# Expert tiles: token numbers in a small tile of their own, biases loaded apart from the matrices and ahead of them

## The chip, the cores and the metric

The kernel runs on one core of one Trainium2 chip. The metric is the device time of one execution in microseconds (us), the median of several runs. The profile is one execution taken by the hardware profiler; its span, 1414.2 us, is close to the median of the runs, 1411.49 us.

## The reference

A network of two layers works on a picture of 2 x 256 x 48 x 48. Only its last part is touched here, a mixture of experts over B*N = 2 * 2304 = 4608 tokens of C = 256 numbers:

```
gate_logits = xf @ Wg + bg
top_w, top_i = top_k(gate_logits, 2);  top_w = softmax(top_w)
w_dense[token, e] = top_w of the expert e, else 0
for e in range(8):
    h = gelu(xf @ W1[e] + b1[e])              # 256 -> 1024
    out += w_dense[:, e] * (h @ W2[e] + b2[e])  # 1024 -> 256
```

Each token goes to two of the eight experts, so 9216 rows of token and expert have to be worked through. Everything is float32.

## The kernel before

The stages ahead (a local attention with a convolution, then a state-space layer with the gate) fill the first 838 us and are not touched. The gate writes each normalised token twice into a table in memory, `xs`, sorted by expert. A row of `xs` has XW = C + E + 1 = 265 numbers: the token's 256, its weight for each of the 8 experts, and in the last column the token's own number.

`experts` works through this table in tiles. A pair tile has 256 rows (2 halves of 128), a single tile 128. There are 36 pair tiles and, among them, 4 single ones; further single tiles stand behind a branch that is only taken when the counts demand it. Two tables computed on the chip (`plan`) say where the rows of each tile begin and which expert they belong to, so the loads use addresses from registers.

For tile i:

- `fetch(i)` (L1752) issues two loads on the queue of SyncE: the rows into `ex` (265 KB for a pair, four buffers) and the whole weights of the expert into `wt` (2184 KB, three buffers). A row of `wt` holds, per partition, W1 (2048 numbers), W2 (2048), then b1 (8), b2 (256) and a mask of the expert (8): WCOL = 4368 in all. The first tile's weights lie in a buffer of their own that is filled long before.
- `turn(i)` (L1767) transposes the rows on TensorE (L895), copies them to `ext` on VectorE (L897), and works out each row's weight: `own` is the product of the row's eight gate weights with the mask from `wt` (L1777), `weight` is their sum (L1781).
- `up(i)` (L1811) is the first matrix: 32 matmuls into PSUM (L1820), and on ScalarE a Gelu with b1 added into `hid` (L1824).
- `weight_sums(i)` (L1793 to L1796) and `hidden_sums(i)` (L1805 to L1808) form on VectorE the sums `ts` and `ss` of blocks that a seven-product scheme for two-by-two blocks needs. `ts` and `ss` have one buffer each.
- `down(i)` (L1837) is the second matrix: for a pair tile the seven products in the order p1, p7, p2, p4, p5, p6, p3, 8 matmuls each (L1859). p7 needs the sum s3, p5 needs s1, p6 needs s2 and p3 needs s4. VectorE then adds the products up into the results `ey` (L1864 to L1870) and adds b2 (L1872). For a single tile, 16 plain matmuls (L1846) and one addition (L1847).
- `finish` (L1826) scales a half's result by its weight on ScalarE (L1829) and adds it to the tokens' rows of `acc` in memory with an indirect DMA on GpSimd (L1831): "the scatter". The rows' numbers are the last column of `ex`, so `ex` stays in use until the scatter has landed.

`run` (L1886) calls them in this order, and loads three tiles ahead:

```
up(i); turn(i + 1); hidden_sums(i); down(i); weight_sums(i + 1); fetch(i + 3)
```

A scheduler places the instructions of each engine in this neighbourhood, and each engine then runs its own list strictly in order; a buffer that is used again makes the instruction that writes it wait for its former readers. The loads on SyncE keep their program order, so a load that waits holds up the loads behind it. The scheduler puts `own` of a tile far forward on VectorE: ahead of the `ts` of the tile before it and of the results of the tile before that.

Of the kernel before, what the change touches and what calls it, by code (L numbers as in the profile page):

```python
# [31 lines left out]
F32 = mybir.dt.float32  # L32
I32 = mybir.dt.int32
AF = mybir.ActivationFunctionType
ALU = mybir.AluOpType
AX = mybir.AxisListType

P = 128
B, C, H, W = 2, 256, 48, 48
N = H * W  # L40
NH = C // P
# [29 lines left out]
E, HID = 8, 1024  # L71
NHC = HID // P
# [5 lines left out]
NUSUAL = E // 2  # L78
NROWS = E * PART + TR
XW = C + E + 1  # L80
WCOL = NH * HID + NHC * C + NHC + C + E
F32_EPS = float(np.finfo(np.float32).eps)


# [30 lines left out]
def bcast(ap, axis, shape):  # L115
    return ap.unsqueeze(axis).to_broadcast(shape)


class Flow:
# [12 lines left out]
    def add(self, key, engine, cost, make, needs=(), takes=(), uses=(), due=0, chain=None, mode=None):  # L132

        self.ops[key] = dict(engine=engine, cost=cost, make=make, needs=[n for n in needs if n], takes=takes,
                             uses=[u for u in uses if u], due=due, chain=chain, mode=mode)
# [87 lines left out]
class Kernel:  # L225
# [1496 lines left out]
    def experts(self, ctx):  # L1722
        nc, ins = self.nc, self.ins
        self.psum(ctx, 4, 2)
        hp = self.pool("eh", 2, ctx)
        ew = self.pool("ew", 3, ctx)
# [4 lines left out]
        fetched, turned, hidden, sums = {}, {}, {}, {}  # L1731
# [19 lines left out]

        def fetch(i):  # L1752
            halves, n = tiles[i]
            x = hp.tile([P, 2, XW], F32, tag="ex", name="ex", bufs=4)[:, :halves]
            if i == 0:
                self.tc.keep_in_program_order(nc.sync.dma_start(x, self.expert_rows(self.xs[0:TR, :])))
                fetched[i] = x, self.first_weights
                return
            at = where[2 - halves]
            row = self.value(at[0:1, 0, n : n + 1], sp, NROWS - TR)  # L1760
            part = self.value(at[0:1, 1, n : n + 1], sp, (E - 1) * P)
            nc.sync.dma_start(x, self.expert_rows(self.xs[bass.ds(row, halves * P), :]))
            wt = ew.tile([P, WCOL], F32, tag="wt", name="wt")
            self.tc.keep_in_program_order(nc.sync.dma_start(wt, ins["We"][bass.ds(part, P), :]))
            fetched[i] = x, wt

        def turn(i):  # L1767

            halves = tiles[i][0]
            x, wt = fetched[i]  # L1770
            xt = hp.tile([P, NH, halves * P], F32, tag="ext", name="ext")
            self.transposes(
                xt.rearrange("p k q -> p (k q)"),
                [x[:, j, k * P : (k + 1) * P] for k in range(NH) for j in range(halves)], nc.vector.tensor_copy,
            )
            own = hp.tile([P, halves, E], F32, tag="own", name="own")
            nc.vector.tensor_tensor(  # L1777
                own, x[:, :, C : C + E], bcast(wt[:, WCOL - E :], 1, [P, halves, E]), ALU.mult
            )
            weight = hp.tile([P, halves], F32, tag="weight", name="weight")  # L1780
            nc.vector.tensor_reduce(weight, own, AX.X, ALU.add)  # L1781
            turned[i] = xt, weight

        def weight_sums(i):

# [24 lines left out]

        def up(i):  # L1811
            rows = tiles[i][0] * P
            xt, wt = turned[i][0], fetched[i][1]
            w1 = wt[:, : NH * HID].rearrange("p (k o) -> p k o", k=NH)
            b1 = wt[:, WCOL - C - NHC - E : WCOL - C - E]
            hid = hidden[i] = hp.tile([P, NHC, rows], F32, tag="hid", name="hid")
            for c in range(NHC):
                ps = self.bank()
                for k in range(NH):
                    nc.tensor.matmul(  # L1820
                        ps[:, :rows], lhsT=w1[:, k, c * P : (c + 1) * P], rhs=xt[:, k, :],
                        start=k == 0, stop=k == NH - 1,
                    )
                nc.scalar.activation(hid[:, c, :], ps[:, :rows], AF.Gelu, bias=b1[:, c : c + 1])  # L1824

        def finish(i, y, j):  # L1826

            x, weight = fetched[i][0], turned[i][1]
            nc.scalar.activation(y, y, AF.Identity, scale=weight[:, j : j + 1])  # L1829
            token = x[:, j, XW - 1 :].bitcast(I32)  # L1830
            put = nc.gpsimd.indirect_dma_start(  # L1831
                self.acc, bass.IndirectOffsetOnAxis(ap=token, axis=0), y, None, compute_op=ALU.add
            )
            self.tc.declare_no_dep(put.ins, group=f"tile{i}", reason="a token has one row of an expert")
            self.tc.add_to_no_dep_group(f"tile{i}", put.ins)

        def down(i):  # L1837
            wt, hid = fetched[i][1], hidden[i]
            w2 = wt[:, NH * HID : NH * HID + NHC * C].rearrange("p (k o) -> p k o", k=NHC)
            b2 = wt[:, WCOL - C - E : WCOL - E]  # L1840
            banks = self.ps2.tile([P, 2, 512], F32, tag="banks", name="po")
            if tiles[i][0] == 1:
                y = hp.tile([P, C], F32, tag="ey", name="ey", bufs=5)
                po = banks[:, 0, :C]
                for c in range(NHC):
                    nc.tensor.matmul(po, lhsT=hid[:, c, :P], rhs=w2[:, c, :], start=c == 0, stop=c == NHC - 1)  # L1846
                nc.vector.tensor_add(y, po, b2)  # L1847
                finish(i, y, 0)
            else:
                v = sums.pop(i)  # L1850
                p = {}

                for n, (name, a, w) in enumerate((
                    (1, "a11", "b11"), (7, "s3", "t3"), (2, "a12", "b21"), (4, "a22", "t4"), (5, "s1", "t1"),
                    (6, "s2", "t2"), (3, "s4", "b22"),
                )):
                    p[name] = banks[:, n // 4, n % 4 * P : (n % 4 + 1) * P]
                    for c in range(NHC // 2):
                        nc.tensor.matmul(p[name], lhsT=v[a][:, c], rhs=v[w][:, c], start=c == 0, stop=c == NHC // 2 - 1)  # L1859
                y0, y1 = (hp.tile([P, C], F32, tag="ey", name="ey", bufs=5) for _ in range(2))  # L1860
                p1, u2, u3, u4 = (hp.tile([P, P], F32, tag=f"u{j}", name=f"u{j}", bufs=1) for j in range(4))
                add = nc.vector.tensor_add
                nc.scalar.copy(p1, p[1])  # L1863
                add(y0[:, :P], p[2], p1)  # L1864
                add(u2, p[6], p1)
                add(u3, p[7], u2)
                add(u4, p[5], u2)
                add(y1[:, :P], p[4], u3)
                add(y1[:, P:], p[5], u3)
                add(y0[:, P:], p[3], u4)  # L1870
                for j, y in enumerate((y0, y1)):
                    add(y, y, b2)  # L1872
                    finish(i, y, j)
            del fetched[i], turned[i], hidden[i]

        fill(0)
        fetch(0)
        where, many = self.plan(plan)
        turn(0)
        for e in range(1, E):  # L1880
            fill(e)
        fetch(1)
        fetch(2)
        weight_sums(0)

        def run(first, end):  # L1886
            for i in range(first, end):
                up(i)
                if i + 1 < end:
                    turn(i + 1)  # L1890
                if tiles[i][0] == 2:
                    hidden_sums(i)
                down(i)
                if i + 1 < end:
                    weight_sums(i + 1)
                if i + 3 < end:
                    fetch(i + 3)
# [3 lines left out]
        with self.tc.If(self.value(many[0:1, 0:1], list(self.nc.engines), NSINGLE) > NUSUAL):  # L1901
            for i in range(usual, usual + 3):
                fetch(i)
            turn(usual)
            run(usual, len(tiles))
# [17 lines left out]
    def run(self):  # L1923
# [33 lines left out]
        nc.vector.tensor_copy(self.taken, self.c["base"])  # L1957
        self.first_weights = self.pool("ew0", 1).tile([P, WCOL], F32, name="wt")
        nc.sync.dma_start(self.first_weights, self.ins["We"][0:P, :])
# [37 lines left out]
def _arrays(i):  # L1997
# [29 lines left out]
        "W_in": w_in, "W_out": at("W_out").T,  # L2027
        "We": experts.reshape(E * P, WCOL),
        "vec": np.concatenate([vec[k] for k in _VEC], axis=1),
# [21 lines left out]
```

## Time and profile before

| | |
|---|---|
| median of 3 runs | 1411.49 us (1408.32 to 1415.42) |
| span of the profiled execution | 1414.2 us |
| TensorE, matmuls | 1269.9 us, 90% |
| VectorE | 1013.5 us, 72% |
| ScalarE | 780.4 us, 55% |
| GpSimd | 531.3 us, 38% |
| up, L1820, 1280 matmuls | 275.5 us |
| `wt` loads | 40 of 2184 KB |
| `ex` loads | 36 of 265 KB, 4 of 132.5 KB |
| scatters, L1831 | 76, 1559 ns each on GpSimd |

The shares are averages over very different stages. The stage in question begins at 838.43 us with the first matmul of `up` and ends for TensorE at 1374 us; behind it `acc` is read back, transposed and written out. What the change is worth has to be read from that stretch alone: which engine runs without a gap there, and which wait ends last in a tile. An engine's wait of many microseconds may cost nothing if another engine is never kept waiting by it. A line is a line of the kernel's program; where one helper serves many places (L895, L897) the names of the tiles tell them apart.

### The profile page before, as it was taken

The page shows a single profiled execution, that of the slowest core. Times are in us where ns is not written, and L with a number is a line of the kernel's source. Part 1 is how long each engine was busy: PE and PEld are TensorE (multiplying, and loading weights), DVE is VectorE, ACT ScalarE, POOL GpSimd, SP SyncE. Part 2 cuts the span into 40 slices and gives each one's busy share as a digit, 9 for nine tenths or more (in the row PEclk, how much of TensorE's full clock was granted, in tenths as well). Part 3 has the DMA queues.
Part 4 walks back from the last instruction along what each step waited for, and adds up shares of the span by engine and source line. Part 5 has one row for each costly group of instructions (what it writes and reads, how often), then busy time and mean ns, then how long its engine had stood idle before and what let it go on. Part 6 is the DMA issues. An engine that isn't in the chain of part 4 may idle for free.

```text
span 1414.2 us, 23686 instructions
## 1 busy us (share of the span) xinstructions
PE 1269.9 (90%) x8144; PEld 1012.9 (72%) x8144; DVE 1013.5 (72%) x2610; ACT 780.4 (55%) x1920; POOL 531.3 (38%) x648
## 2 busy tenths in 40 slices
PE   5999999998998899999988539998999999999983
PEld 4566767666666566666665429997998999998983
DVE  4999999997788889899978636654645645655653
ACT  2688877897987777777866212332332332432320
POOL 5213030111466777778676831221222222221220
PEclk9999999997999999999999859999999999999996
DMA  7321413121332233324243147666566667666628
GB/s 285 107 88 46 138 38 105 37 64 65 116 99 82 68 90 107 101 93 120 82 127 100 57 134 279 209 194 214 177 217 225 180 218 232 196 208 219 203 50 275
DMA packets 100442, 199.54 MB, mean 141 GB/s; under 512 B 10059, under 2 KB 86044, under 8 KB 94876
## 3 DMA queue, kind: packets, MB, share of 16 engines
q1 hardware_dynamic: 80540, 171.57, 36.4%
q0 software_dynamic: 14400, 19.74, 6.6%
q10 hardware_dynamic: 5380, 6.69, 1.4%
q8 instruction: 66, 1.08, 0.3%
q14 instruction: 56, 0.46, 0.1%
HBM read 158.71 MB, written 44.18 MB: 143 GB/s over the span
## 4 chain that ended last, share of the span: by engine, by line
PE 38%; DVE 15%; DMA 14%; ACT 3%; issue 3%; POOL 2%; another core or an unknown queue 0%; SPq 0%; DVEq 0%; ACTq 0%; POOLq 0%
PE bank L1820 11%; PE po L1859 10%; DMA wt<-in_We 7%; DMA acc<-ey,ex 5%; PE bank L909 4%; PE zbank L909 3%; PE bank L1420 2%; DVE xc L1106 2%; PE bank L895 1%; PE bank L1359 1%; PE bank L1402 1%; DVE mt L1322 1%; ACT mt L1314 1%; DVE y L1410 1%; POOL xs L1629 1%
## 5 line engine op out<-in xcount | busy, mean ns | idle before, releaser
L1820 PE MATMUL bank<-ext,wt 128*128 128x256 f32 (+1 forms) x1280 | 275.5, 373 | 10.0 <-ACT hid L1824 9.2
L1831 POOL DMA_INDIRECT acc<-ey,ex x76 | 118.5, 1559 | 435.0 <-ACT ey L1829 394.8
L1820 PEld LDWEIGHTS bank<-ext,wt 128*128 128x128 f32 x1280 | 233.0, 192 | 41.7 <-ACT hid L1824 11.7
L1824 ACT ACTIVATE hid<-bank,wt 128x256 f32<-128x256 f32 (+1 forms) x320 | 143.0, 462 | 83.0 <-PE bank L1820 79.0
L1863 ACT COPY u<-po 128x128 f32<-128x128 f32 x36 | 9.6, 266 | 226.6 <-PE po L1859 226.6
L1859 PE MATMUL po<-ts,ss 128*128 128x128 f32 x864 | 108.4, 275 | 0.0
L1859 PEld LDWEIGHTS po<-ts,ss 128*128 128x128 f32 x864 | 102.6, 192 | 0.0
L585 DVE SCALAR_TENSOR_TENSOR x<-hid,w2r,x 128x1128 f32<-128x1128 f32 (+3 forms) x72 | 99.9, 1392 | 0.4 <-ACT hid L579 0.2
L909 PE MATMUL bank<-xn,win 128*128 128x387 f32 x240 | 94.3, 517 | 1.1 <-DVE lg L1445 1.0
L1777 DVE TENSOR_TENSOR own<-ex,wt 128x16 f32<-128x16 f32 (+1 forms) x40 | 6.9, 173 | 122.9 <-DMA wt<-in_We 114.8
L674 POOL COPY kp<-kp 128x10 f32<-128x10 f32 (+1 forms) x60 | 23.4, 390 | 190.2 <-DVE kp L667 190.2
L793 ACT ACTIVATE prob<-prob,top 128x308 f32<-128x308 f32 x144 | 78.2, 549 | 17.4 <-DVE top L782 17.0
L1314 ACT ACTIVATE mt<-mt,cum 128x128 f32<-128x128 f32 x288 | 87.4, 392 | 0.0
L1106 DVE SCALAR_TENSOR_TENSOR xc<-bank,vec,xc 128x384 f32<-128x384 f32 x144 | 85.1, 605 | 2.4 <-ACT xc L1095 2.2
L909 PE MATMUL zbank<-xn,win 128*128 128x384 f32 x192 | 77.6, 529 | 4.2 <-ACT z L1216 4.2
L1629 POOL DMA_INDIRECT xs<-u,rows x72 | 71.9, 999 | 22.5 <-issue 16.7
L1859 PE MATMUL po<-wt,hid 128*128 128x128 f32 x576 | 77.5, 278 | 0.0
L1420 PE MATMUL bank<-wout,y 128*128 128x264 f32 x288 | 72.9, 398 | 2.6 <-DVE ss L1435 1.3
L1859 PEld LDWEIGHTS po<-wt,hid 128*128 128x128 f32 x576 | 71.7, 195 | 0.1
L824 PE MATMUL bank<-pt,val 110*64 110x128 f32 (+1 forms) x864 | 69.4, 278 | 0.8 <-ACT pt L814 0.8
L799 ACT ACTIVATE prob<-prob,rden 128x308 f32<-128x308 f32 x144 | 67.7, 547 | 4.3 <-DVE rden L848 4.2
L824 PEld LDWEIGHTS bank<-pt,val 110*64 110x64 f32 (+1 forms) x864 | 58.7, 136 | 14.7 <-issue 10.2
(288 smaller groups left out, 2982.7 us busy)
## 6 DMA issues: line engine op xcount, KB each, us to landing
wt<-in_We SPq DMA_DIRECT2D x40, 2184.0 KB
mt<-decays SPq DMA_DIRECT2D x36, 512.0 KB
ex<-xs SPq DMA_DIRECT2D x36, 265.0 KB
rd<-decays SPq DMA_DIRECT2D x68, 128.0 KB
val<-vtab SPq DMA_DIRECT2D x72, 110.0 KB
vraster<-vout SPq DMA_DIRECT2D x18, 256.0 KB
acc<-x SPq DMA_DIRECT2D x36, 128.0 KB
vtab<-vraster SPq DMA_DIRECT2D x12, 304.0 KB
```

The costliest lines, as they stand in the source:

```text
L585: nc.vector.scalar_tensor_tensor(dst, src, w[:, k : k + 1], dst, ALU.mult, ALU.add)
L793: nc.scalar.activation(t, t, AF.Exp, bias=T["top", c][:, a : a + 1], scale=-1.0, accum_out=T["den", c][:, a : a + 1])
L824: nc.tensor.matmul(po[j * HD : (j + 1) * HD, :P], lhsT=T["val", c][:nk, i, a * HD : (a + 1) * HD], rhs=T["pt", key][:nk, j, i, :], start=i ...
L909: self.nc.tensor.matmul(ps, lhsT=lhs(k), rhs=rhs(k), start=k == 0, stop=k == NH - 1)
L1106: nc.vector.scalar_tensor_tensor(out(), T["bank", ("cv", at)][:, i : i + TB], wc[:, i : i + 1], out(), ALU.mult, ALU.add)
L1314: nc.scalar.activation(t, t, AF.Relu, bias=at_s, scale=-1.0)
L1420: nc.tensor.matmul(ps[:, : C + E], lhsT=T["y", c][:, m, :], rhs=self.l1["wout"][:, m, :], start=m == 0, stop=m == NZ - 1,)
L1629: ins = nc.gpsimd.indirect_dma_start(self.xs, bass.IndirectOffsetOnAxis(ap=of("rows")[:, i, q : q + 1], axis=0), T["u2", g][:, i, :], None,)
L1820: nc.tensor.matmul(ps[:, :rows], lhsT=w1[:, k, c * P : (c + 1) * P], rhs=xt[:, k, :], start=k == 0, stop=k == NH - 1,)
L1824: nc.scalar.activation(hid[:, c, :], ps[:, :rows], AF.Gelu, bias=b1[:, c : c + 1])
L1831: put = nc.gpsimd.indirect_dma_start(self.acc, bass.IndirectOffsetOnAxis(ap=token, axis=0), y, None, compute_op=ALU.add)
L1859: nc.tensor.matmul(p[name], lhsT=v[a][:, c], rhs=v[w][:, c], start=c == 0, stop=c == NHC // 2 - 1)
```

## The change

The tile `wt` is split. The matrices (WMAT = 4096 numbers a partition, 2048 KB) stay in `wt`, and b1, b2 and the mask (272 numbers, 136 KB) go into a new tile `bt` with four buffers, which is loaded ahead of the matrices. `own`, the Gelu's bias and the addition of b2 now read `bt`. So `wt` is free again after the last matmul of its tile, and the work on weights and biases doesn't hang on the large load.

The numbers of the tokens are copied on VectorE from the last column of `ex` into a tile `token` with three buffers, and the scatter takes them from there. So `ex` is free after the transposes, `own` and that copy, and gets three buffers in place of four, which makes room for `bt`: one buffer of `ex` less is 2120 bytes a partition, `wt` is 3 x 1088 smaller, `bt` takes 4 x 1088.

```diff
 def fetch(i):
-            x = hp.tile([P, 2, XW], F32, tag="ex", name="ex", bufs=4)[:, :halves]
+            x = hp.tile([P, 2, XW], F32, tag="ex", name="ex", bufs=3)[:, :halves]
...
             nc.sync.dma_start(x, self.expert_rows(self.xs[bass.ds(row, halves * P), :]))
-            wt = ew.tile([P, WCOL], F32, tag="wt", name="wt")
-            self.tc.keep_in_program_order(nc.sync.dma_start(wt, ins["We"][bass.ds(part, P), :]))
-            fetched[i] = x, wt
+
+            bt = hp.tile([P, WCOL - WMAT], F32, tag="bt", name="bt", bufs=4)
+            self.tc.keep_in_program_order(nc.sync.dma_start(bt, ins["We"][bass.ds(part, P), WMAT:]))
+            wt = ew.tile([P, WMAT], F32, tag="wt", name="wt")
+            self.tc.keep_in_program_order(nc.sync.dma_start(wt, ins["We"][bass.ds(part, P), :WMAT]))
+            fetched[i] = x, wt, bt
...
 def turn(i):
-                own, x[:, :, C : C + E], bcast(wt[:, WCOL - E :], 1, [P, halves, E]), ALU.mult
+                own, x[:, :, C : C + E], bcast(bt[:, NHC + C :], 1, [P, halves, E]), ALU.mult
...
-            turned[i] = xt, weight
+            token = hp.tile([P, halves], I32, tag="token", name="token", bufs=3)
+            nc.vector.tensor_copy(token, x[:, :, XW - 1].bitcast(I32))
+            turned[i] = xt, weight, token
...
 def up(i):
-                nc.scalar.activation(hid[:, c, :], ps[:, :rows], AF.Gelu, bias=b1[:, c : c + 1])
+                nc.scalar.activation(hid[:, c, :], ps[:, :rows], AF.Gelu, bias=bt[:, c : c + 1])
...
 def finish(i, y, j):
-            token = x[:, j, XW - 1 :].bitcast(I32)
...
-                self.acc, bass.IndirectOffsetOnAxis(ap=token, axis=0), y, None, compute_op=ALU.add
+                self.acc, bass.IndirectOffsetOnAxis(ap=token[:, j : j + 1], axis=0), y, None, compute_op=ALU.add
...
 def down(i):
-            b2 = wt[:, WCOL - C - E : WCOL - E]
+            b2 = bt[:, NHC : NHC + C]
```

The matmuls and the sums of blocks are the same, in the same order on TensorE.

More of the change, by code (lines that the diff above doesn't have):

```diff
@@ L80 @@
 XW = C + E + 1
-WCOL = NH * HID + NHC * C + NHC + C + E
+WMAT = NH * HID + NHC * C
+WCOL = WMAT + NHC + C + E
 F32_EPS = float(np.finfo(np.float32).eps)
@@ L1753, in fetch @@
             halves, n = tiles[i]
-            x = hp.tile([P, 2, XW], F32, tag="ex", name="ex", bufs=4)[:, :halves]
+            x = hp.tile([P, 2, XW], F32, tag="ex", name="ex", bufs=3)[:, :halves]
             if i == 0:
                 self.tc.keep_in_program_order(nc.sync.dma_start(x, self.expert_rows(self.xs[0:TR, :])))
-                fetched[i] = x, self.first_weights
+                fetched[i] = x, self.first_weights[:, :WMAT], self.first_weights[:, WMAT:]
                 return
@@ L1762, in fetch @@
             nc.sync.dma_start(x, self.expert_rows(self.xs[bass.ds(row, halves * P), :]))
-            wt = ew.tile([P, WCOL], F32, tag="wt", name="wt")
-            self.tc.keep_in_program_order(nc.sync.dma_start(wt, ins["We"][bass.ds(part, P), :]))
-            fetched[i] = x, wt
+            bt = hp.tile([P, WCOL - WMAT], F32, tag="bt", name="bt", bufs=4)
[3 more added lines that the diff above has]
+            fetched[i] = x, wt, bt
         def turn(i):
             halves = tiles[i][0]
-            x, wt = fetched[i]
+            x, wt, bt = fetched[i]
             xt = hp.tile([P, NH, halves * P], F32, tag="ext", name="ext")
@@ L1812, in up @@
             rows = tiles[i][0] * P
-            xt, wt = turned[i][0], fetched[i][1]
+            xt, wt, bt = turned[i][0], *fetched[i][1:]
             w1 = wt[:, : NH * HID].rearrange("p (k o) -> p k o", k=NH)
-            b1 = wt[:, WCOL - C - NHC - E : WCOL - C - E]
             hid = hidden[i] = hp.tile([P, NHC, rows], F32, tag="hid", name="hid")
@@ L1823, in up @@
                     )
-                nc.scalar.activation(hid[:, c, :], ps[:, :rows], AF.Gelu, bias=b1[:, c : c + 1])
+                nc.scalar.activation(hid[:, c, :], ps[:, :rows], AF.Gelu, bias=bt[:, c : c + 1])
         def finish(i, y, j):
-            x, weight = fetched[i][0], turned[i][1]
+            _, weight, token = turned[i]
             nc.scalar.activation(y, y, AF.Identity, scale=weight[:, j : j + 1])
-            token = x[:, j, XW - 1 :].bitcast(I32)
             put = nc.gpsimd.indirect_dma_start(
-                self.acc, bass.IndirectOffsetOnAxis(ap=token, axis=0), y, None, compute_op=ALU.add
+                self.acc, bass.IndirectOffsetOnAxis(ap=token[:, j : j + 1], axis=0), y, None, compute_op=ALU.add
             )
@@ L1837, in down @@
         def down(i):
-            wt, hid = fetched[i][1], hidden[i]
+            wt, bt, hid = *fetched[i][1:], hidden[i]
             w2 = wt[:, NH * HID : NH * HID + NHC * C].rearrange("p (k o) -> p k o", k=NHC)
-            b2 = wt[:, WCOL - C - E : WCOL - E]
+            b2 = bt[:, NHC : NHC + C]
             banks = self.ps2.tile([P, 2, 512], F32, tag="banks", name="po")
```

## The prediction

> **What bounds the kernel now.** I read the page's slices, then stretches of the expert stage (838 to 1374 us), then its waits, then one tile in order of time, and last the traffic of each DMA queue in that tile. The stretches first (PE, PEld, DVE, ACT, POOL busy; granted clock; DMA share; GB/s):
>
> ```profile
> 1000.00:1100.00 100.00, 98.07 (x663) 91.58 (x662) 53.45 (x131) 32.42 (x77) 20.24 (x13) 0.98 0.65 206
> 1100.00:1200.00 100.00, 98.99 (x670) 92.28 (x669) 56.75 (x142) 35.27 (x84) 23.33 (x15) 1.00 0.68 215
> 1200.00:1300.00 100.00, 98.65 (x660) 91.76 (x659) 55.30 (x140) 36.11 (x86) 22.08 (x15) 1.00 0.66 205
> ```
>
> TensorE is the bound. A pair tile costs it 13.6 us (up 6.91, transposes 0.44, down 6.25 in the chain of waits), a single tile 7.47. So 36 x 13.6 + 4 x 7.47 = 519 us of 536 are unavoidable. Of the other 17, 3 are the slow first tile (up in 9.73 instead of 6.91); about 13 can be won. The waits, 860 to 1345 us, of TensorE, VectorE and the DMA queue (total, times, longest):
>
> ```profile
> PE bank L1820 <- ACT hid L1824: 9.0, 4, 4.7
> ...
> DVE own L1777 <- DMA wt<-in_We: 114.8, 34, 9.2
> ...
> SPq L1762 <- DMA acc<-ey,ex: 331.1, 41, 17.5
> SPq L1764 <- DVE ey L1872: 90.7, 32, 4.1
> ```
>
> VectorE waits for a matrix load in nearly each tile, but only four of the delays reach TensorE, each around a single tile: 4.7+1.9+1.0+1.4 us, and after the two long ones the clock falls to 0.50, for about 2 us more each. That is the 13.
>
> One tile. E is the end of the last bias addition (L1872, 1102.82); D the end of the last down matmul (1098.55).
>
> ```profile
> 1098.78 0.17 DVE L1777 TENSOR_TENSOR own<-ex,wt 128x16 f32<-128x16 f32 x1 [3.76 <-DMA wt<-in_We]
> 1102.07 0.75 DVE L1872 TENSOR_TENSOR ey<-ey,wt 128x256 f32<-128x256 f32 x2
> 1106.00 0.69 DVE L1806 TENSOR_TENSOR ss<-hid 128x512 f32<-128x512 f32 x1 [1.49 <-ACT hid L1824]
> 1107.93 0.69 DVE L1808 TENSOR_TENSOR ss<-hid,ss 128x512 f32<-128x512 f32 x1
> ...
> 1103.03 0.33 SPq L1764 DMA_DIRECT2D wt<-in_We  x1
> 1112.76 0.39 SPq L1762 DMA_DIRECT2D ex<-xs  x1
> ...
> 1103.30 1.56 POOL L1831 DMA_INDIRECT acc<-ey,ex  x1 [10.82 <-ACT ey L1829]
> 1105.16 1.55 POOL L1831 DMA_INDIRECT acc<-ey,ex  x1 [0.30 <-ACT hid L1824]
> ```
>
> The matrix load leaves at E+0.2, since the bias that L1872 reads lies in the same tile. The next `ex` leaves at 1112.76, when this tile's scatter has landed: **R = E+9.9** (other tiles up to E+11.1). Why so late shows in the queues' traffic (packets, MB, share), the first line for 1108.03 to 1110.03, the last two for 1110.03 to 1112.03:
>
> ```profile
> q1 hardware_dynamic: 44, 0.77, 95.7%
> q0 software_dynamic: 30, 0.03, 9.5%
> ...
> q0 software_dynamic: 258, 0.23, 74.3%
> q1 hardware_dynamic: 19, 0.05, 7.5%
> ```
>
> q1 carries the matrices, q0 the scatter. Until the matrices are through, 7.2 us after their issue, the scatter's 1 KB rows hardly move.
>
> [...] POOL ended at 1106.71, R came 6.0 later. [...] The trace has 0.50 after a gap of 4.72, but after one of 1.93 us too, and 1.00 after one of 1.01.
>
> **The change part by part.**
>
> 1. `own` reads `bt`, not `wt`. In the built program it still stands ahead of the next tile's `ts` and this tile's results on VectorE. `bt` (136 KB) of tile i+3 waits for L1872 of tile i-1, so is issued at that tile's E and has about 9.5 us until `own`; behind a matrix load and `ex` on q1 it needs some 7. The 114.8 us of waits go, and with them the 13 us.
> 2. `wt` is released by the last matmul: issue at D+0.25 = E-2.8 instead of E+0.2. Nobody waited for it but `own`: worth nothing by itself.
> 3. `ex` has 3 buffers and is free after its transposes, `own` and the token copy; it no longer waits for the scatter (331.1 us). SyncE's time: hidden. But `ex` (265 KB, about 1.0 us of all engines) now follows directly behind `wt` on q1, in the scatter's time.
> 4. 39 more DMA issues of 0.33 us: SyncE waits most of the time, nothing. Bytes are the same.
> 5. 40 token copies; nearest row `weight`, 0.17 us: 7 us of a VectorE that is 55% busy, nothing.
> 6. **The new wait.** `token` has 3 buffers, so the copy for tile n+3 overwrites what the scatter of tile n reads and waits until it has landed, on VectorE instead of SyncE. In the built program the copy stands between L1805 (s3) of tile n+1 and its s1, s2, s4, with the `ext` copy among them: under 1 us after tile n's E. Behind it is all that tile n+1's down phase needs: p5 needs s1, p6 s2, p3 s4.
>
> When does the copy hurt? Up, transposes and p1, p7, p2, p4 (four of seven in 6.25) take 6.91+0.44+3.57 = 10.9, p5 is due at D+10.9, p6 at 11.8, p3 at 12.7. Unhindered, E = D+3.1 (L1793 follows p6, and L1872 ends 3.94 after its start), so at E+7.7, 8.6, 9.5. By the rows above s1 to s4 takes 2.6 us; with the copy, 2.8 from R to the last, 2.1 to s2. So R up to **E+6.5** is free, and each us beyond lengthens the tile by one: tile = R-E+7.1.
>
> R after the change is what the trace does not show. Floor: the last tile, without loads, had E = 1376.81 and the next issue behind its scatter at 1383.11: **E+6.3**. Ceiling: matrices through at E-2.8+6.8 (7.2 less 6% of bytes) = E+4.0; then what the scatter needed behind them before, 2.5 to 3.3 us (in most tiles 9.7 to 10.5 after the issue, less 7.2), then `ex` and `bt` ahead of it, 1.0+0.5: **E+8.8**. I take the middle, 7.55: 1.05 us a tile. Of 36 pair tiles, the first three meet no full buffer, the last three have no copy behind them, and some lie at a single tile: 28 x 1.05 = +29. At a single tile its own scatter follows the pair's and the next copy waits for it: I count up to 1.8 us for each of four, +6. With -13: 1411.5+29+6-13 = **1434**.
>
> **The rivals.**
>
> - *The copy waits and costs (forecast), 0.56:* R from E+7.0 to 8.4, time 1419 to 1458. For it: the built order, and a scatter that starves behind q1's loads. Against: the matrices now start 3 us earlier against it.
> - *The scatter lands in time, 0.22:* R below E+6.6. The waits go and nothing replaces them: 1411.5-13 = 1398, or 1403 if single tiles still stall. For it: floor 6.3 is below 6.5. Against: `ex` and `bt` run just then.
> - *Both cancel, 0.12:* R about E+6.8, 28 x 0.3+4-13: 1411.
> - *Full starvation and clock, 0.10:* R at E+8.8 is 28 x 2.3 = 64, +6-13 = 1469; TensorE's gap then comes near the 1.93 us that halved the clock, and 1 us more in each tile makes 1497. Against: until now the scatter took its share when small packets ran.
>
> **The numbers.** Forecast and starvation are slower: 0.66. The second is faster: 0.22. Same: 0.12. The range, 1400 to 1464, reaches from most of the in-time case to the forecast's upper end, and leaves out the starvation case and the best of the faster one.
>
> **What would show it.** Right: VectorE waits for "DMA acc" ahead of the token copy in nearly each tile, some 4 to 6 us; TensorE has gaps at L1859 ahead of `ss`, about 1 us a tile; `own` waits for nothing; matrices issue about 3 us ahead of E; SyncE no longer waits for the scatter ahead of `ex`. Wrong: tiles at 13.6 us with the token wait ending before TensorE is due (second case); or `own` waiting for `bt`, which would shift the stall to the loads' order; or TensorE waiting for a thing not named here.

## The result and the profile after

The changed kernel takes 1464.98 us (median of 4 runs, 1458.72 to 1469.84) against 1409.9 us (4 runs, 1406.99 to 1415.42) for the kernel before: ratio 1.0383, 95% interval 1.0331 to 1.0436. That is slower, as forecast, but by 55 us where 22 were forecast, and just beyond the upper end of the range (1464).

The same three stretches as before, in the kernel after (columns: stretch, its length, busy us and instruction counts of PE, PEld, DVE, ACT, POOL; then granted clock, DMA share, GB/s):

```profile
1000.00:1100.00 100.00, 91.67 (x594) 83.67 (x592) 48.09 (x127) 31.31 (x75) 20.24 (x13) 0.98 0.60 192
1100.00:1200.00 100.00, 89.27 (x562) 80.87 (x563) 50.44 (x132) 30.37 (x73) 20.22 (x13) 0.97 0.60 192
1200.00:1300.00 100.00, 97.32 (x659) 89.63 (x658) 57.02 (x146) 33.14 (x79) 20.16 (x13) 1.00 0.57 181
```

TensorE has come down from 98 or 99 to between 89 and 97. The first two stretches hold a single tile each and show a clock of 0.98 and 0.97; the third holds none, loses 2.7 us and keeps 1.00. That is the first hint of two losses of different kinds. The waits of the expert stage (total us, times, longest us):

```profile
DVE token L1787 <- DMA acc<-ey,token: 216.8, 37, 10.5
...
PE bank L1825 <- ACT hid L1829: 21.4, 4, 5.8
PE po L1863 <- DVE ss L1812: 17.4, 20, 1.8
...
SPq L1768 <- PE po L1863: 353.8, 32, 13.3
```

The wait of VectorE for the matrix load is gone (`own` appears with no wait at all), and SyncE no longer waits for the scatter ahead of `ex`. In their place VectorE waits for the scatter ahead of 37 of the 40 token copies. TensorE is reached in two places: 20 short gaps at L1863, none over 1.8 us, and four at L1825, of 5.4 us on average.

One regular tile, that is, a pair tile that doesn't stand directly ahead of a single one. E is the end of the last b2 addition (the first line: 1107.55), R the moment at which the scatter has landed, read from the start of the copy that waited for it:

```profile
1106.80 0.75 DVE L1876 TENSOR_TENSOR ey<-ey,bt 128x256 f32<-128x256 f32 x2
...
1116.28 0.17 DVE L1787 COPY token<-ex 128x2 int32<-128x2 int32 x1 [6.89 <-DMA acc<-ey,token]
1116.36 0.68 DVE L1812 TENSOR_TENSOR ss<-hid 128x512 f32<-128x512 f32 x1
...
1117.10 2.36 PE L1863 MATMUL po<-ts,ss 128*128 128x128 f32 x16 [1.77 <-DVE ss L1812]
...
1104.44 0.33 SPq L1768 DMA_DIRECT2D wt<-in_We  x1
1105.60 0.38 SPq L1763 DMA_DIRECT2D ex<-xs  x1
1107.66 0.33 SPq L1766 DMA_DIRECT2D bt<-in_We  x1
```

The matrices leave at E-3.1. The copy waits until R = E+8.73, the sum for p5 (L1812) stands right behind it, and TensorE waits 1.77 us for that sum. Over the 28 regular pair tiles (the first and the last three left out), R averages E+7.48 (6.8 to 8.73).

Why R is that late shows in the next tile, whose matrices left at 1120.4: the first of its two scatter instructions, then the traffic by queue (packets, MB, share of the DMA engines), first 1124.4 to 1127, then 1127 to 1129, then 1129 to 1131:

```profile
1124.12 1.56 POOL L1835 DMA_INDIRECT acc<-ey,token  x1 [12.52 <-ACT ey L1834]
...
q1 hardware_dynamic: 67, 1.08, 97.5%
...
q1 hardware_dynamic: 432, 0.46, 65.5%
q0 software_dynamic: 117, 0.11, 37.6%
...
q0 software_dynamic: 171, 0.15, 50.1%
q1 hardware_dynamic: 2, 0.00, 0.2%
```

While q1 carries matrices, q0 (the scatter) moves nothing, though GpSimd's two scatter instructions begin at 1124.12 and 1125.98. By the single packets of the trace, the first of the scatter starts at 1128.09, 0.14 us after the last matrix packet has ended and 3.97 us after the first instruction began. By then q1 is down to the small packets of `ex` and `bt` and has moved about 290 of the 432 that the view counts. In the last three tiles of this kernel, with no matrix load beside them, the first packet starts 2.12 to 2.13 us after the instruction, so here it is 1.8 us late.

And the surroundings of one single tile, which the prediction dealt with too briefly:

```profile
959.30 0.17 DVE L1787 COPY token<-ex 128x2 int32<-128x2 int32 x1 [10.50 <-DMA acc<-ey,token]
959.38 0.42 DVE L1851 TENSOR_TENSOR ey<-po,bt 128x256 f32<-128x256 f32 x1
...
959.83 0.51 ACT L1834 ACTIVATE ey<-ey,weight 128x256 f32<-128x256 f32 x1 [11.37 <-DVE ey L1851]
...
960.75 5.45 PE L1825 MATMUL bank<-ext,wt 128*128 128x256 f32 x16 [5.77 <-ACT hid L1829]
...
944.09 0.33 SPq L1768 DMA_DIRECT2D wt<-in_We  x1
...
951.56 0.33 SPq L1768 DMA_DIRECT2D wt<-in_We  x1
```

Read it from the bottom up. A single tile ends 7.5 us after the pair tile ahead of it, so a second matrix load (951.56) leaves only 7.5 us after the first (944.09). The scatter of the pair, issued on GpSimd from 947.82 to 951.2, runs into both. So R of the pair is 12.1 us behind its E of 947.2, not 7.5. The copy holds the single tile's own result (L1851) behind it on VectorE. ScalarE waits 11.37 us to scale that result, and the next tile's Gelus stand behind the scaling. With no Gelu, no PSUM bank comes free, and TensorE stops in the middle of `up`. When it goes on, 16 matmuls take 5.45 us; 16 of the same shape took 3.62 just ahead (the granted clock is 0.50 from 960.75 to 964 us).

### The profile page after: what moved, and what is told of

Same layout as the page of the kernel before. It is cut to its first block, busy times and chain, and to the rows that moved or that the text cites. A ratio compares the mean times of both kernels' runs of the same rounds, so it can differ in the third digit from the quotient of the medians.

```text
span 1463.9 us, 23771 instructions
## 1 busy us (share of the span) xinstructions
PE 1290.2 (88%) x8144; PEld 1021.4 (70%) x8144; DVE 1015.8 (69%) x2650; ACT 779.5 (53%) x1920; POOL 531.3 (36%) x648
## 4 chain that ended last, share of the span: by engine, by line
PE 33%; DMA 17%; DVE 13%; POOL 5%; issue 4%; ACT 3%; SPq 1%; another core or an unknown queue 0%; DVEq 0%; ACTq 0%; POOLq 0%
DMA acc<-ey,token 12%; PE bank L1825 9%; PE po L1863 8%; PE bank L910 4%; POOL acc L1835 3%; PE zbank L910 2%; PE bank L1421 2%; DMA ex<-xs 2%; PE bank L1403 1%; PE bank L1360 1%; DVE xc L1107 1%; DVE mt L1323 1%; DVE ss L1812 1%; ACT ey L1834 1%; POOL xs L1630 1%
## 5 line engine op out<-in xcount | busy, mean ns | idle before, releaser
L1825 PE MATMUL bank<-ext,wt 128*128 128x256 f32 (+1 forms) x1280 | 282.1, 380 | 22.4 <-ACT hid L1829 21.4
L1835 POOL DMA_INDIRECT acc<-ey,token x76 | 118.3, 1557 | 483.1 <-ACT ey L1834 442.4
L1825 PEld LDWEIGHTS bank<-ext,wt 128*128 128x128 f32 x1280 | 238.6, 197 | 55.9 <-ACT hid L1829 23.0
L1829 ACT ACTIVATE hid<-bank,bt 128x256 f32<-128x256 f32 (+1 forms) x312 | 141.4, 460 | 93.9 <-PE bank L1825 88.8
L1787 DVE COPY token<-ex 128x2 int32<-128x2 int32 (+1 forms) x40 | 6.7, 167 | 216.8 <-DMA acc<-ey,token 216.8
L1863 PE MATMUL po<-ts,ss 128*128 128x128 f32 x864 | 117.4, 281 | 18.9 <-DVE ss L1812 17.4
L1863 PEld LDWEIGHTS po<-ts,ss 128*128 128x128 f32 x864 | 103.9, 191 | 28.6 <-DVE ss L1812 23.1
L1863 PE MATMUL po<-wt,hid 128*128 128x128 f32 x576 | 76.1, 275 | 0.0
L1863 PEld LDWEIGHTS po<-wt,hid 128*128 128x128 f32 x576 | 70.2, 192 | 0.1
L825 PEld LDWEIGHTS bank<-pt,val 110*64 110x64 f32 (+1 forms) x864 | 59.2, 137 | 14.7 <-issue 9.6
```

Of the source, the lines that this page charges most:

```text
L825: nc.tensor.matmul(po[j * HD : (j + 1) * HD, :P], lhsT=T["val", c][:nk, i, a * HD : (a + 1) * HD], rhs=T["pt", key][:nk, j, i, :], start=i ...
L1825: nc.tensor.matmul(ps[:, :rows], lhsT=w1[:, k, c * P : (c + 1) * P], rhs=xt[:, k, :], start=k == 0, stop=k == NH - 1,)
L1835: put = nc.gpsimd.indirect_dma_start(self.acc, bass.IndirectOffsetOnAxis(ap=token[:, j : j + 1], axis=0), y, None, compute_op=ALU.add)
```

## The experiments

All times are medians; the ratio is to the kernel before, run on the same chip.

| kernel | us | ratio (95%) |
|---|---|---|
| e1: 6 token buffers | 1402.61 | 0.9899 (0.9864 to 0.9934) |
| e2: 3 buffers at single tiles only | 1433.28 | 1.0119 (1.0077 to 1.0161) |
| e3: 3 buffers at pair tiles only | 1434.24 | 1.0141 (1.0092 to 1.0191) |
| e4: token part alone | 1618.27 | 1.1423 (1.1387 to 1.1459) |
| e5: no matrix loads | 1404.59 | 0.9943 (0.9919 to 0.9967) |
| e6: split part alone | 1424.18 | 1.0066 (1.0044 to 1.0089) |
| e7: copy on GpSimd | 1403.79 | 0.9902 (0.9859 to 0.9945) |
| e8: e2, one load less at a single | 1432.74 | 1.0148 (1.0111 to 1.0185) |
| e9: e2, two loads less at a single | 1413.52 | 0.9978 (0.9952 to 1.0003) |
| e10: 4 token buffers | 1404.6 | 0.9914 (0.9892 to 0.9935) |

**e1, is it the reuse of the token buffer?**

```diff
-            token = hp.tile([P, halves], I32, tag="token", name="token", bufs=3)
+            token = hp.tile([P, halves], I32, tag="token", name="token", bufs=6)
```

> The changed kernel with six token buffers in place of three, so that the copy waits for scatters that landed long ago; all else as in the change. Theory A (the copy on VectorE waits for the last tile's scatter, and this wait is the whole loss): VectorE no longer waits for acc ahead of the copy, TensorE has no gaps ahead of L1863 or at single tiles, the 66 us lost in the expert stage of the changed kernel fall to about 5: 1397 to 1405 us, faster than before by some 0.7%. Rival B (splitting the load, with 5600 more small packets and ex and bt beside the scatter, costs by itself): stays above 1440. Rival C (ex with three buffers comes too late): stays above 1430, with waits for ex.

Measured: 1402.61 us. No copy waits for a scatter, and TensorE is busy without a break in each of four stretches from 900 to 1300 us, for instance:

```profile
1100.00:1200.00 100.00, 100.00 (x675) 93.46 (x674) 57.01 (x148) 36.44 (x86) 23.33 (x15) 1.00 0.68 218
```

The whole loss goes away with three small buffers, and what remains is the gain of about 14 us over the kernel before (1% of 1416) that was forecast as 13. The traffic is the same. With more buffers the scheduler also puts the copy elsewhere, just ahead of `own`; e2, e3, e7 and e10 deal with that.

**e2 and e3, which copies cost what?** In both, most tiles get a token tile of their own. In e2 only the 8 copies that stand around single tiles reuse the tile of three tiles before; in e3 only the others do.

```diff
-            token = hp.tile([P, halves], I32, tag="token", name="token", bufs=3)
+            old = i - 3 in tags and (any(tiles[n][0] == 1 for n in (i - 3, i - 2) if n < usual))
+            tags[i] = tags[i - 3] if old else f"token{i}"
+            token = hp.tile([P, halves], I32, tag=tags[i], name="token", bufs=1)
```

(e3: `not any(...)`.)

> The changed kernel, but only those copies reuse a token buffer three tiles back that stand at a single tile (8 of them); all other tiles have a token buffer of their own. Theory A with the split that the changed kernel's trace gives (four stretches around single tiles lose 31 us together, 28 other tiles 32 us, against a base of about 1397): 1425 to 1431 us, with four gaps of about 5 us at L1825 and a halved clock after each, and none ahead of L1863. Rival D (the losses at single tiles come only because the pairs ahead of them are already late): 1400 to 1410, gaps at the single tiles under 2 us.

> The changed kernel, but the copies at single tiles have a token buffer of their own, and all others reuse one three tiles back. Theory A: 1397 + 28 tiles x 1.15 = 1429, 1424 to 1434 us; R, the landing of the scatter, stays 7 to 8.7 us after the tile's last bias addition, and no gap at L1825. Rival D: 1445 or more, since the pairs carry the loss at the single tiles.

Measured: 1433.28 and 1434.24 us, that is 2.20% and 2.42% of the kernel before more than e1, together 4.6%; the changed kernel has 4.8% more than e1. The two parts add up, and they are of one size: eight copies cost as much as all the others. TensorE's waits, of e2 and then of e3:

```profile
PE bank L1827 <- ACT hid L1831: 22.2, 4, 5.8
```

```profile
PE po L1865 <- DVE ss L1814: 17.5, 24, 1.8
```

Each has one of the two kinds of gap alone. In e3 the clock is 1.00 in each stretch of 100 us from 900 to 1300, in e2 0.97: the long gaps cost clock, the short ones don't.

**e4, the token part without the split.** The kernel before, with the copy into `token` (3 buffers), `ex` in 3 buffers, and biases still in `wt`.

> The kernel before with the token part of the change alone: token copy with three buffers, ex with three; weights and biases stay in one load, so the load leaves only after the last bias addition, E. Theory A, with tile = (R-E)+7.1: the load runs fully against the scatter, R was E+10.4 in the kernel before and ex now follows directly on the same queue (+1.0), so a tile takes 17.5 to 18.5 us, 28 x (3.9 to 4.9) = 109 to 137 more, and single tiles lose again 30 or more: 1520 to 1570 us. Rival B (the split is what costs): close to the kernel before, under 1420.

Measured: 1618.27 us, far above what was expected. The waits of its longer expert stage, then one matmul group in order of time:

```profile
DVE token L1783 <- DMA acc<-ey,token: 322.6, 37, 9.9
...
PE po L1860 <- DVE ss L1808: 115.3, 28, 6.2
```

```profile
1112.94 3.78 PE L1860 MATMUL po<-ts,ss 128*128 128x128 f32 x16 [4.37 <-DVE ss L1808]
```

R was about where it was expected, E+10.0 to E+11.7 (11.0 on average), since the matrices now leave at E and not at E-3. What was missed is the clock: after a gap of 4.37 us, 16 matmuls take 3.78 us (2.05 in the kernel after, behind a gap of 0.81), the mean clock is 0.85 to 0.90 in stretches of 100 us, and a regular tile takes 20.1 us on average, about 2 us more than its R alone would make it. So within the change the split is worth much more than nothing: with it the matrices leave 3 us earlier, and the scatter lands 3.5 us earlier (E+7.48 against E+11.0).

**e5, is the scatter late because of the matrices?** All tiles use the first expert's matrices, which lie on the chip; `ex` and `bt` are loaded as before.

```diff
-            wt = ew.tile([P, WMAT], F32, tag="wt", name="wt")
-            self.tc.keep_in_program_order(nc.sync.dma_start(wt, ins["We"][bass.ds(part, P), :WMAT]))
+            wt = self.first_weights[:, :WMAT]
```

> The changed kernel, three token buffers and the same waits, but the matrices are not loaded: all tiles compute with the first expert's (so the results are not the reference's); ex and bt are loaded as in the change. Theory A (the wait costs only because the scatter starves behind the matrix loads): the scatter lands 6.3 to 7.0 us after the last bias addition, pair tiles take 13.6 to 14.1 us, the gaps at single tiles fall under 2 us each: 0.5 to 1.0% faster than before, about 1400 to 1408 us, although VectorE still waits at the copy. Rival E (the wait costs by itself, whatever runs beside it, through POOL and the landing): stays above 1430.

Measured: 1404.59 us, R = E+6.3 to E+7.1, regular tiles of 13.6 to 13.8 us in 24 cases of 28 and of 14.3 us at most.

```profile
DVE token L1786 <- DMA acc<-ey,token: 139.9, 37, 5.2
```

The copy still stands in the same place and VectorE still waits 140 us in 37 copies, but TensorE is hardly kept waiting (two gaps of 0.2 us). A wait costs only what it lasts beyond the moment at which the work behind it is due. It bears out the prediction's "R up to E+6.5 is free" closely: tiles with R up to E+6.4 take 13.6 us, and those with a later R take R-E+7.2.

**e6, the split without the token part.** The kernel before with `bt` in 4 buffers; `ex` keeps 4 buffers and the scatter reads the numbers from `ex` (one buffer of the last stage's output tile is given up for the room).

> The changed kernel without its token part: the scatter reads the numbers from ex, ex has four buffers again (the output stage has five buffers of o in place of six, to make room). Theory A: own waits for nothing, nothing replaces that wait on VectorE, SyncE waits for the scatter ahead of ex as before: 0.8 to 1.1% faster than before, about 1398 to 1404, like the kernel with six token buffers. Rival B (the split costs): slower than before.

Measured: 1424.18 us, slower than before, where 1398 to 1404 were expected.

```profile
SPq L1763 <- DMA acc<-ey,ex: 350.0, 40, 16.5
```

```profile
DVE own L1781 <- DMA bt<-in_We: 151.5, 34, 8.7
```

`bt` stands behind `ex` in SyncE's queue, and `ex` waits for the scatter as it did before. So `own` now waits for `bt` in 34 tiles, longer than it waited for `wt` before (114.8 us), and TensorE's gaps add up to 15.5 us (6 gaps), 12.1 of it in four gaps around single tiles, where these four were 9.0. (The buffer given up at the end costs little: what comes after the last matmul of the stage takes 40.5 us, against 40.1.) The two parts of the change need each other: without the copy the small load comes late, without the split the scatter does.

**e7, the same wait on another engine.**

```diff
-            nc.vector.tensor_copy(token, x[:, :, XW - 1].bitcast(I32))
+            nc.gpsimd.tensor_copy(token, x[:, :, XW - 1].bitcast(I32))
```

> The changed kernel with the token copy on GpSimd, three token buffers as in the change: the same wait for the same scatter, in another engine's list, where only the next scatter stands behind it. Theory A (it is the place of the wait that costs): 0.6 to 1.0% faster than before, 1401 to 1407. Rival F (three buffers are too few wherever the copy stands, since the token itself is late): above 1430.

Measured: 1403.79 us, with three buffers and TensorE busy in every stretch. GpSimd waits for the scatter instead (75.6 us in 24 copies are put down to it), and nothing that is due stands behind it there.

**e8 and e9, is it the second matrix load at a single tile?** Both start from e2. In e8 the tile three behind each single tile uses the first expert's matrices, so that one load falls away; in e9 the tile after it does too.

```diff
-            self.tc.keep_in_program_order(nc.sync.dma_start(wt, ins["We"][bass.ds(part, P), :WMAT]))
+            if i < usual and tiles[i - 3][0] == 1:
+                wt = self.first_weights[:, :WMAT]
+            else:
+                self.tc.keep_in_program_order(nc.sync.dma_start(wt, ins["We"][bass.ds(part, P), :WMAT]))
```

(e9: `tiles[i - 3][0] == 1 or tiles[i - 4][0] == 1`.)

> The kernel that waits at the single tiles alone (e2), without the matrix load that leaves at the end of a single tile (that tile, four of 40, computes with the first expert's matrices, so its results are not the reference's). Theory A' (at a single tile the next matrix load leaves 7.5 us after the last one, while the pair's scatter is still waiting, and starves it again, R = E+12): the scatter of the pair ahead lands at E+7 to 8, the gaps of 5.5 us at L1825 fall under 2 us and the clock stays: 4 to 12 us above the kernel with six token buffers, against 31 in e2, so about 1406 to 1414. Rival G (the two waits in a row at a single tile cost in any case): stays within 5 us of e2, 1428 or more.

Measured: 1432.74 us, no gain on e2. At the first single tile R of the pair ahead fell from E+12.0 to E+9.1, but R of the single tile rose from E+4.5 to E+9.3; the other three are alike. The order of time shows why:

```profile
946.35 0.33 SPq L1771 DMA_DIRECT2D wt<-in_We  x1
...
946.48 1.56 POOL L1840 DMA_INDIRECT acc<-ey,token  x1 [6.44 <-ACT ey L1839]
```

With a buffer free, the next matrix load, which in e2 leaves at 963.83, leaves at 946.35, right ahead of the single tile's own scatter. One load was gone, but the next one had moved up, and the delay with it from one scatter to the other. That led to e9:

> Like e8 (the token buffer is reused only at the 8 copies around single tiles), but the two matrix loads that would follow the end of a single tile are both left out; the two tiles concerned use the first expert's matrices, so their part of the output is another one. In e8 the load left out at 941.7 us was followed by the next one at 946.35 us, 0.13 us ahead of the single tile's own scatter, instead of at 963.8 us: the load was moved from the pair's scatter onto the single's. Theory A (a copy costs what the scatter is late, and the scatter is late because of a matrix load beside it): now both scatters meet no matrix load, R falls to about E+6 to E+8 for the pair ahead and E+4 to E+6 for the single, the TensorE gaps ahead of up and of down behind single tiles (5.8 us at 3 buffers, 4.5 us in e8) fall under 2 us, and the time to 1405 to 1415 us. Rival B (at a single tile the tile is so short that any landing time stalls it; loads don't matter): the gaps stay at 4 to 6 us and the time at 1428 to 1436 us.

Measured: 1413.52 us. R is E+7.9 to E+9.2 for the pair ahead and E+4.6 for the single tile, TensorE's longest gap 3.0 us:

```profile
PE bank L1830 <- ACT hid L1834: 9.7, 4, 3.0
```

That is 20 of the 31 us that e2 lost (the expert stage takes 521.9 us in the profile of e1, 555.2 in e2, 535.0 in e9). So most of the loss at single tiles comes from a scatter that runs into two matrix loads. The rest stays since R is still late: the four gaps are 2.4 us on average at an R of E+8.7, and 5.35 us at E+11.7 in the changed kernel, so in both cases the gap is R-E-6.3. R up to E+6.3 would be free here too. Why R is E+8.7 and not E+7.5 as in a regular tile was not tested; with no matrix load to hold it up, the `ex` load of the next tile leaves at 937.92, right beside the scatter (begun at 937.23), where in e2 it left at 942.87.

**e10, how many buffers does it take?** Four in place of three.

> The changed kernel with 4 token buffers in place of 3, nothing else. Theory A: a copy then waits for the scatter of one tile earlier, which has had a whole tile more (13.6 us, or 7.5 us where a single lies between) to land; R of 6.8 to 12 us after E then lies ahead of the copy, there is no wait for the scatter (or under 10 us of it in all, at singles), TensorE is busy in every stretch, and the time equals that of 6 buffers, 1400 to 1406 us. Rival B (what 6 buffers won came from the scheduler's other placing of the copy): with 4 buffers the copy stands where it stood with 3 and some wait stays: 1410 to 1440 us.

Measured: 1404.6 us. The time is as expected, but not the waits:

```profile
1098.20 0.69 DVE L1814 TENSOR_TENSOR ss<-hid,ss 128x512 f32<-128x512 f32 x1
1099.15 0.17 DVE L1787 COPY token<-ex 128x2 int32<-128x2 int32 x1 [0.25 <-DMA acc<-ey,token]
```

28 copies still wait, 47.8 us in all, and for the scatter that was issued last, as with 3 buffers: the scheduler has used the fourth buffer to put each copy a tile earlier, now behind the last sum s4 (L1814) and ahead of `own`. There R = E+7.2 has almost passed anyway, and what comes behind is due later. Around single tiles, where R is as late as E+12.7, copies still wait up to 7.1 us, and all that reaches TensorE is two gaps of 2.0 us together. So the expectation was wrong in saying that the copy would wait for an older scatter; it is the place that pays, as in e7.

## Why the prediction was wrong in size

The direction, the mechanism and most of the steps held:

- **Step 1** (`own` no longer waits, 13 us won): held. `own` waits for nothing, and e1, where nothing is lost, shows the gain: 14 us.
- **Step 2** (earlier release of `wt`: worth nothing by itself): true of waits for `wt`, but e4 shows what it does for R: without it the scatter lands 3.5 us later and the kernel takes 1618 us. The prediction did use the earlier start in its bound of R.
- **Steps 3 to 5** (SyncE freed, more issues, copies of 0.17 us): no trace of a cost of their own; what the `ex` and `bt` packets beside the scatter may cost is part of the measured R.
- **Step 6, pair tiles**: held. R was put at E+7.55, and it is E+7.48 on average over 28 tiles; since 7.55 was no more than the middle between two bounds 2.5 us apart, so close a hit is in part luck. A tile was to take R-E+7.1 and takes R-E+7.2. The 28 were to cost 28 x 1.05 = 29 us; counted from E to E they average 14.7 us instead of 13.6, which is 28 x 1.09 = 31. e3 has 2.4%, 34 us, with these waits alone.
- **Step 6, single tiles: the step that failed.** It counted "up to 1.8 us for each of four, +6". The four stretches from the pair tile ahead over the single tile to the end of the next pair tile take 28.8, 28.0, 29.4 and 28.8 us, where 7.47 + 13.6 = 21.07 is what the matmuls need: 31 us lost. e2 has 2.2%, 31 us, with these waits alone.

The corrected sum is 1409.9 + 31 + 31 - 13 = 1459, 6 us under what was measured. The single-tile term was too small for two reasons. R was carried over from regular tiles: ahead of a single tile two matrix loads leave 7.5 us apart and R becomes E+11.3 to E+12.1, so each gap is R-E-6.3, 5.35 us on average. e9, where two loads are missing, has 20 of the 31 us back. And the clock was reckoned with only in the starvation rival: after these gaps 16 matmuls take 5.4 to 6.3 us instead of 3.62, on average 2.2 us more. 4 x (5.35 + 2.2) = 30 of the 31. The kernel before had the sign of it: its two longest gaps, 4.7 and 1.9 us, lay around single tiles with the same releaser, the Gelus, and were followed by a granted clock of 0.50.

Of the rivals, "the scatter lands in time" is what e5 shows when the matrices are off the queue. "Full starvation" came near the measured time (1469), but for another reason: R in regular tiles lay below its ceiling of E+8.8 on average, and e3 keeps its clock at 1.00.

## What to carry to other kernels

A buffer that is freed by a slow indirect DMA should be reused late enough, or by an engine with nothing urgent behind it: here one more buffer of two numbers per partition (e10), or another engine for a copy of 0.17 us (e7), turned 4% slower into 1% faster (e1, with 6, is as fast as these within the spread of the runs). When a wait moves from one engine's list to another's, ask what stands behind it in every kind of tile, not just in the regular one; four irregular tiles cost as much here as 28 regular ones. And a load that is taken away may only let the next one go sooner, against the very transfer that was to be spared (e8).

## What the runs showed of the hardware

- A scatter started later beside a large load. In the changed kernel its first packet starts 2.12 to 2.13 us after the first instruction begins in the four single tiles, where the last matrix load left 8.2 to 9.1 us ahead of it, and in the last three tiles, which have no load beside them. In the regular tiles of the changed kernel, where the matrices leave 3.7 to 4.7 us ahead of the instruction, it starts after 2.6 to 4.0 us; in the pair tiles of the kernel before that have a load beside them, where the matrices leave 0.26 to 0.45 us ahead of it, after 4.7 to 5.3. GpSimd's own instruction takes 1.55 to 1.7 us in both kernels, so it is not slowed; what holds up the first packet is not shown.
- When both queues move, the scatter's share of the bytes was small: in the kernel before, 30 packets of the scatter, 1 KB each, beside 44 of 17 KB in the 2 us from 1108.03 on that the prediction shows. By number the scatter has two packets for every three of the load, but it moves 0.03 MB of 0.80.
- The length of a gap in TensorE's work did not settle by itself whether the clock fell. In e9 the same 16 matmuls (3.62 us at a granted clock of 1.00) took 3.72 us after gaps of 1.63 and 2.62 us, but 5.33 and 5.41 us after 2.48 and 2.96. The mean clock is 1.00 in the stretches around the first two (1150 to 1190 and 1040 to 1080 us), 0.97 and 0.96 in those around the other two (930 to 980 and 1255 to 1300). The gap of 2.62 us:

```profile
1053.80 3.72 PE L1830 MATMUL bank<-ext,wt 128*128 128x256 f32 x16 [2.62 <-ACT hid L1834]
```

In the kernel before, a gap of 1.93 us was followed by a clock of 0.50 (1075.8 to 1079.1 us). The gaps in regular tiles of the changed kernel, up to 1.77 us, cost no clock: it is 1.00 from 1080.4 to 1192.9 us, where five of them lie, the longest among them. What decides beside the length is not shown here.
